# One left-over block product by seven products: a half-width node in the feed-forward stage of a recurrent block, with its sums on GpSimd

## The chip, the core and the metric

The kernel runs on one NeuronCore of a Trainium2 chip. The metric is the device time of one execution in microseconds (us); smaller is better. Beside the times of plain runs there is one profiled execution, whose trace names every instruction by the line of the kernel that issued it (L783 is line 783). The engines are TensorE (PE in the profile, its weight loads PEld), VectorE (DVE), ScalarE (ACT), GpSimd (POOL) and SyncE (SP, which issues most DMAs).

## The reference

Input x is 8 x 1024 x 512 in float32 (8 batches). All arithmetic is float32.

```python
xn = layernorm(x)
s  = attention(xn)            # recurrent, three decays, gated; times Wo and a scale
gate = xn @ lut[gate_idx].T   # 512 -> 1376
up   = xn @ lut[up_idx].T     # 512 -> 1376
h    = silu(gate) * up
g    = silu(h @ lut[down_idx].T)   # 1376 -> 512
out  = x + s * g
```

The change lies in the products `gate` and `up`. Their 1376 output columns are 11 tiles: ten of 128 (0 to 9) and one of 96 (10).

## The kernel before

Phase 1 normalizes x, runs the attention and writes to HBM, for each batch, x transposed and its block sums (`xs_d`); on the way it looks up the three weight matrices and writes their block sums to HBM as well. Phase 2 goes through the eight batches. For each one it computes gate and up (`quads`, and `single` for tile 10), then the down projection (`down`) and the output. In batch 0 `single` comes before `quads`; in batches 1 to 7 it comes after.

**Products of blocks.** Gate and up together are a 2 x 2 block product in the scheme of Strassen and Winograd: seven block products, numbered 1 to 7, in place of eight, with sums of the results. Each of the seven is itself done by seven products of smaller blocks. Such an inner scheme is a `Node`: it has four results in four PSUM banks (`t[0]` to `t[3]`, of the roles s11, s12, s21, sE) and adds its seven products into them. A quad is four output tiles. For the two quads (tiles 0 to 3 and 4 to 7) a node holds two weight tiles side by side, and goes through the block products 1, 6, 5, 7, 2, 3, 4 in seven nodes, `(1, 1)` to `(4, 4)`.

**The pair.** Tiles 8 and 9 are a pair. Here the two halves of a node are two different block products: `(1, 6)`, `(5, 7)` and `(2, 3)`, in that order. The seventh one left, block product 4, is no node. `Fourth` computes it without an inner scheme: two results of two matmuls of 512 columns each (L826), which DVE adds to the pair's `u3` (L835). It needs the x blocks of 4 as they were, which is why `restore` (L853) brings the second x block of product 4 back after the last node of the second quad.

**The order.** Every engine runs its instructions in the order in which they are traced (`keep_order`). The loop of `quads` interleaves each node with the first two steps of the one that follows, so that PE has the matmuls of the follower while ACT and DVE work on the results of the node:

```python
node.sixth()               # PE product 6; ACT copies t1 to t2 (L805); DVE t1 += e (L806)
node.product(0, 2); empty(node.t, 0)
if following: following.first()          # PE product 1; ACT copies t0 to t1 (L794)
node.seventh(); empty(node.t, 3)         # PE product 7, needs L805; DVE t3 = t2 + e (L810)
node.product(1, 3); empty(node.t, 1)     # PE product 3, needs L806
if following: following.fifth(); following.fifth_copy()   # PE product 5; ACT L801
if node.restores: restore(...)           # a DMA from ACT's queue
node.product(2, 4); empty(node.t, 2)     # PE product 4, needs L810
if after: after()                        # GpSimd
```

The matmuls of a node are L783: two matmuls of 256 columns a product, and each float32 matmul shows as two instructions of PE, so a product is four. `Fourth` stands in this loop as the follower of `(2, 3)`: its two results take the places of `first` and `fifth`; the first of its DVE adds (L835) stands ahead of L810, the second ahead of the adds for t2. After `(2, 3)` comes `single` (L721 to L758), or in batch 0 the first node of `down` (`DownNode`: L1037, L1059, L1066, L1070).

**What `empty` and `after` do for the pair.** Node (1, 6): ACT copies to p1 (L915), DVE adds to u2 (L916). Node (5, 7): ACT copies to e5 (L919), DVE adds to u3 (L920), GpSimd adds e5 to u2 (L921); after it GpSimd adds u3 to e5 (L931). Node (2, 3): DVE adds into p1 (L924) and into h (L926, needs L921), ACT applies Silu to both (L925, L927); after it GpSimd multiplies h by u3 and by e5 (L936).

**Weights.** A ring of three slots holds the weights of a node (L774 for the quads, L777 twice for a pair's node, 448 KB each; L819 twice for `Fourth`, 128 KB each; L721 for `single`; L1028 for `down`). The DMA of one starts when the one three places earlier has been read for the last time.

**Sums for the down projection.** `at_last` puts up to six DVE sums (L1005) into this loop in batch 0, two of them in node (5, 7) and three in (2, 3), one ahead of L810; in the other batches they lie in `single`.

Of the kernel before, what the change touches and what calls it, by code (L numbers as in the profile page):

```python
# [9 lines left out]
F32 = mybir.dt.float32  # L10
# [4 lines left out]
ALU = mybir.AluOpType  # L15
AX = mybir.AxisListType

P = 128
# [30 lines left out]
def recurrent_block(ctx: ExitStack, tc, x, wq, wk, wv, wo, wg, decay_logits, out_scale, lut, gidx, uidx, didx, out):  # L49
# [19 lines left out]
    nc = tc.nc  # L69
# [5 lines left out]
    U = 512  # L75
# [5 lines left out]
    NK = (NO - 1) // 2  # L81
    NQ = NO // 4
# [7 lines left out]
    wgu_d = [dram.tile([P, 14, m], F32, name=f"wgud{o}", tag=f"wgud{o}") for o, (_, m) in enumerate(OCH)]  # L90
# [42 lines left out]
    def defer(parts, issue):  # L133
        later.append([parts, issue])
# [111 lines left out]
    def ffn_weights(build, pool, pair_pool):  # L246
# [9 lines left out]
        def gate_up(o):  # L256
            s, m = OCH[o]
            n = 2 * NV * m
            idx = build.tile([P, NB], I32, name="idx", tag="idx", bufs=2)
            iv = idx[:, :n].rearrange("p (a b) -> p a b", b=m)  # L260
            gs, us = (src[:, s : s + m].rearrange("(c p) b -> p c b", p=P) for src in (gidx, uidx))
            nc.sync.dma_start(out=iv[:, 2:6, :], in_=gs)
            nc.sync.dma_start(out=iv[:, 0:2, :], in_=us[:, 0:2, :])
            nc.sync.dma_start(out=iv[:, 6:8, :], in_=us[:, 2:4, :])
            yield
            wf = pool.tile([P, 2 * NB], F32, name="wgu", tag="wgu", bufs=2)
            yield from look_up(build, wf[:, :n], idx[:, :n], P, n)
            w = wf[:, : 2 * n].rearrange("p (k two m) -> p k two m", two=2, m=m)
            a21, a11, a12, a22, s1, s2, s3, s4 = (w[:, k] for k in range(8))
            nc.gpsimd.tensor_tensor(s1, a21, a22, ALU.add)  # L270
            nc.gpsimd.tensor_tensor(s2, s1, a11, ALU.subtract)
            yield
            nc.gpsimd.tensor_tensor(s3, a11, a21, ALU.subtract)
            nc.gpsimd.tensor_tensor(s4, a12, s2, ALU.subtract)
            wide = wf[:, 2 * m : 2 * n].rearrange("p (a b) -> p a b", b=m)
            if o >= 4 * NQ:
                defer(3, lambda: nc.sync.dma_start(out=wgu_d[o], in_=wide))
            if o >= 2 * NK:
                return
            if o % 2 == 0:  # L280
                upper.append(w[:, 1:])
                return
            up, low = upper.pop(), w[:, 1:]
            to = quad_d[o // 4][:, :, o // 2 % 2, :].rearrange("p k (t m) -> p k t m", m=P)
            pair = pair_pool.tile([P, 7, 4, P], F32, name="pair", tag="pair")
            nc.sync.dma_start(out=to[:, :, 0:2, :], in_=up)
            defer(3, lambda: nc.sync.dma_start(out=to[:, :, 2, :], in_=low[:, :, 1, :]))
            b21, b22, b11, b12 = low[:, :, 0], low[:, :, 1], up[:, :, 0], up[:, :, 1]
            nc.gpsimd.tensor_tensor(pair[:, :, 0], b21, b22, ALU.add)
            yield  # L290
            nc.gpsimd.tensor_tensor(pair[:, :, 1], pair[:, :, 0], b11, ALU.subtract)
            yield
            nc.gpsimd.tensor_tensor(pair[:, :, 2], b11, b21, ALU.subtract)
            yield
            nc.gpsimd.tensor_tensor(pair[:, :, 3], b12, pair[:, :, 1], ALU.subtract)
            defer(4, lambda: nc.sync.dma_start(out=to[:, :, 3:7, :], in_=pair))
            for _ in range(3):
                yield
# [377 lines left out]
    W_OF = {1: 0, 2: 1, 4: 2, 5: 3, 6: 4, 7: 5, 3: 6}  # L676
    X_OF = {1: 0, 2: 1, 3: 2, 5: 3, 6: 4, 7: 5, 4: 6}
    D_OF = {1: 0, 7: 1, 2: 2, 3: 3, 5: 4, 6: 5, 4: 6}
    H = U // 2
    ORDER = (1, 6, 5, 7, 2, 3, 4)  # L680

    def phase_2():
        with (
# [12 lines left out]
            def bank(role, name):  # L696
                return psp.tile([P, U], F32, name=name, tag=role)
# [62 lines left out]
            class Node:  # L760
# [2 lines left out]

                def __init__(self, b, q, ks, xs):
                    self.ks, self.xs = ks, xs

                    self.restores = ks if q == NQ else (4,) if (q, ks) == (NQ - 1, (4, 4)) else ()
                    name = f"{b}_{q}_{ks[0]}"  # L770
                    self.w = ring.tile([P, 2, 7, P], F32, name=f"wq{name}", tag="wr")
                    w = self.w.rearrange("p a t m -> p a (t m)")
                    if q < NQ:
                        nc.sync.dma_start(out=w, in_=quad_d[q][:, W_OF[ks[0]], :, :])  # L774
                    else:
                        for a, k in enumerate(ks):
                            nc.sync.dma_start(out=w[:, a, :], in_=quad_d[q][:, W_OF[k], 0, :])  # L777
                    self.t = [bank(r, f"{r}{name}") for r in ("s11", "s12", "s21", "sE")]
                    self.name = f"e{name}"

                def product(self, n, i, start=False):
                    for a in range(2):
                        nc.tensor.matmul(  # L783
                            self.t[n][:, ts(a, H)],
                            lhsT=self.w[:, a, (0, 1, 6, 2, 3, 4, 5)[i - 1], :],
                            rhs=self.xs[:, X_OF[self.ks[a]], D_OF[i], :],
                            start=start and a == 0,
                            stop=False,
                            skip_group_check=True,
                        )  # L790

                def first(self):
                    self.product(0, 1, True)
                    nc.scalar.copy(self.t[1], self.t[0])  # L794

                def fifth(self):
                    self.product(3, 5, True)
                    self.e = tmp.tile([P, U], F32, name=self.name, tag="e")

                def fifth_copy(self):  # L800
                    nc.scalar.copy(self.e, self.t[3])  # L801
# [6 lines left out]
                def seventh(self):  # L808
                    self.product(2, 7)
                    nc.vector.tensor_tensor(self.t[3], self.t[2], self.e, ALU.add)  # L810

            class Fourth:


                def __init__(self, b, xs, u3):
                    self.b, self.xs, self.u3 = b, xs, u3
                    self.w = ring.tile([P, 14, P], F32, name=f"w4{b}", tag="wr")
                    for r in range(2):
                        nc.sync.dma_start(  # L819
                            out=self.w[:, ts(r, 2), :], in_=wgu_d[4 * NQ + r][:, ts(W_OF[4], 2), :]  # L820
                        )

                def product(self, r, role):
                    ps = bank(role, f"{role}{self.b}_4_{r}")
                    for n in range(2):
                        nc.tensor.matmul(  # L826
                            ps,
                            lhsT=self.w[:, 2 * r + n, :],
                            rhs=self.xs[:, X_OF[4], ts(n, 2), :],
                            start=n == 0,  # L830
                            stop=n == 1,
                            skip_group_check=True,
                        )
                    o = self.u3[:, ts(r, 2), :]
                    return lambda: nc.vector.tensor_tensor(o, ps.rearrange("p (a t) -> p a t", a=2), o, ALU.add)  # L835

                def first(self):
                    self.product(0, "s11")()

                def fifth(self):  # L840
                    self.add = self.product(1, "sE")

                def fifth_copy(self):
                    self.add()

            def quads(b, xs, h, sums, at_last):

# [53 lines left out]
                def pair_steps():  # L901
# [2 lines left out]
                        (t[:, :, :H], t[:, :, H:])  # L904
                        for t in (tmp.tile([P, 4, U], F32, name=f"{k}{b}_l", tag=k) for k in ("p1", "u2"))
                    )
                    room[0] = u3

                    def of_h(half, n):
                        r, c = divmod(n, 2)  # L910
                        t = half * U + c * H
                        return h[:, 4 * NQ + r, t : t + H]
# [20 lines left out]
                    def after_23():  # L933
                        for half, other in ((0, u3), (1, e5)):
                            for n in (0, 3, 1, 2):
                                nc.gpsimd.tensor_tensor(of_h(half, n), of_h(half, n), other[:, n], ALU.mult)  # L936

                    yield (1, 6), node_16, None
                    yield (5, 7), node_57, after_57
                    yield (2, 3), node_23, after_23  # L940

                room = [None]
                def every():
                    for q in range(NQ):
                        for ks, empty, after in steps(q):
                            yield Node(b, q, ks, xs), empty, after
                    for ks, empty, after in pair_steps():
                        yield Node(b, NQ, ks, xs), empty, after
                    yield Fourth(b, xs, room[0]), None, None
                    yield None, None, None  # L950

                todo = every()
# [288 lines left out]
            xs = room_for_x(0)  # L1241
# [92 lines left out]
```

## Time and profile before

| | |
|---|---|
| median of 3 runs | 2119.46 us (2119.22 to 2119.74) |
| the profiled execution | 2119.36 us, its span 2117.6 us |
| PE busy | 2109.2 us, 100% of the span |
| PEld busy | 1678.6 us, 79% |
| DVE, POOL, ACT busy | 1409.2, 1021.2, 929.4 us |
| HBM traffic | 282.87 MB read, 76.55 MB written |
| granted TensorE clock | 1.00 |

Busy is the time in which an engine has an instruction in work. The span runs from the first to the last instruction of the core; 1.76 us of the profiled execution's time lie outside it. A row of groups gives line, engine, operation, output<-inputs, shape and count, then busy us, mean ns of one, and the idle time of the engine ahead of them with what ended it.

### The profile page before, as it was taken

To read this page: it belongs to the slowest core of one execution; us is meant where nothing else is said; L and a number is where in the kernel's file an instruction comes from. 1 tells how busy PE (TensorE), PEld (TensorE's weight loads), DVE (VectorE), ACT (ScalarE), POOL (GpSimd) and SP (SyncE) were. 2 spreads that over 40 slices of the span, in tenths; PEclk is the share of its full clock that TensorE was granted. 3 is DMA by queue.
4 is the path that set the end of the run, shared out by engine and by line. 5 is a ranking of instruction groups with operands and counts; after the bars stand their busy time and mean duration, and the time that the engine had idled before them with its cause. 6 is when DMAs were issued, how large, how long until landed. Compare 5 with 4: busy or idle time off the path is not lost.

```text
span 2117.6 us, 31134 instructions
## 1 busy us (share of the span) xinstructions
PE 2109.2 (100%) x11306; PEld 1678.6 (79%) x11306; DVE 1409.2 (67%) x2150; ACT 929.4 (44%) x2083; POOL 1021.2 (48%) x1046
## 2 busy tenths in 40 slices
PE   9999999999999999999999999999999999999999
PEld 6666666666678888887879888887978888797877
DVE  6889888678545774576567556656755665675557
ACT  3666666666434414423441442344145324423531
POOL 2554565253354537416642752655275255527432
PEclk9999999999999999999999999999999999999999
DMA  7556557565464644464455446444544634464442
GB/s 195 158 176 160 190 174 169 181 129 177 110 252 153 240 168 153 156 236 140 146 195 185 151 148 245 139 147 172 208 151 154 246 123 155 165 218 148 152 154 109
DMA packets 164271, 361.45 MB, mean 171 GB/s; under 512 B 52083, under 2 KB 90230, under 8 KB 163094
## 3 DMA queue, kind: packets, MB, share of 16 engines
q1 hardware_dynamic: 149702, 336.12, 48.7%
q0 software_dynamic: 4480, 14.68, 1.7%
q10 hardware_dynamic: 9936, 8.66, 1.4%
q8 instruction: 90, 1.47, 0.3%
q14 instruction: 63, 0.52, 0.1%
HBM read 282.87 MB, written 76.55 MB: 170 GB/s over the span
## 4 chain that ended last, share of the span: by engine, by line
PE 98%; DVE 1%; DMA 1%; POOL 0%; issue 0%; ACTq 0%; ACT 0%; SPq 0%; POOLq 0%; DVEq 0%
PE s L783 33%; PE pq L455 10%; PE pv L418 8%; PE sE L783 6%; PE s12d L1037 5%; PE s21d L1037 5%; PE s11d L1037 5%; PE po L583 4%; PE fs L731 3%; PE pd L1145 3%; PE ps L1152 3%; PE sEd L1037 2%; PE psc L561 2%; PE pu L569 2%; PE pt L411 1%; PE fsE L731 1%
## 5 line engine op out<-in xcount | busy, mean ns | idle before, releaser
L783 PE MATMUL s<-xs,wq 128*128 128x256 f32 x3264 | 731.2, 379 | 0.0
L783 PEld LDWEIGHTS s<-xs,wq 128*128 128x128 f32 x3264 | 619.6, 190 | 95.8 <-issue 8.1
L806 DVE TENSOR_TENSOR s<-s,e 128x512 f32<-128x512 f32 x136 | 95.1, 699 | 204.1 <-ACT s L805 204.0
L455 PE MATMUL pq<-xnT,wqk_sb 128*128 128x512 f32 x512 | 230.3, 592 | 0.0
L1116 POOL TENSOR_TENSOR cu<-cu 128x256 f32<-128x256 f32 x32 | 34.8, 1088 | 306.7 <-DVE cl L1115 306.7
L418 PE MATMUL pv<-wvg_sb,xnT 128*128 128x387 f32 x512 | 177.6, 489 | 0.3 <-DMA wvg_sb<-in_wv 0.3
L714 POOL TENSOR_TENSOR xs<-xs 128x256 f32<-128x256 f32 x224 | 170.8, 789 | 4.5
L455 PEld LDWEIGHTS pq<-xnT,wqk_sb 128*128 128x128 f32 x512 | 92.4, 190 | 92.1 <-issue 91.8
L810 DVE TENSOR_TENSOR sE<-s,e 128x512 f32<-128x512 f32 x136 | 95.0, 699 | 104.9 <-PE s L783 104.9
L874 POOL TENSOR_TENSOR u<-u,e 128x512 f32<-128x512 f32 x64 | 79.9, 1270 | 148.7 <-DVE u L870 130.2
L801 ACT COPY e<-sE 128x512 f32<-128x512 f32 x136 | 79.6, 585 | 138.8 <-PE sE L783 138.5
L783 PE MATMUL sE<-xs,wq 128*128 128x256 f32 x544 | 139.6, 379 | 0.0
L397 POOL TENSOR_SCALAR rstd<-rstd 128x1 f32<-128x1 f32 x56 | 27.8, 497 | 229.6 <-ACT junk L396 229.0
L418 PEld LDWEIGHTS pv<-wvg_sb,xnT 128*128 128x128 f32 x512 | 92.7, 190 | 54.8 <-issue 2.4
L878 POOL TENSOR_TENSOR h<-h,u 128x512 f32<-128x512 f32 x64 | 80.1, 1272 | 113.1 <-DVE u L885 103.5
L794 ACT COPY s<-s 128x512 f32<-128x512 f32 x136 | 77.5, 570 | 109.2 <-PE s L783 105.1
L805 ACT COPY s<-s 128x512 f32<-128x512 f32 x136 | 77.5, 570 | 97.6 <-PE s L783 97.6
L1037 PE MATMUL s12d<-wdd,z 128*128 128x128 f32 x896 | 118.5, 275 | 0.6 <-ACT s12d L1059 0.6
L783 PEld LDWEIGHTS sE<-xs,wq 128*128 128x128 f32 x544 | 103.4, 190 | 14.0
L1037 PEld LDWEIGHTS s12d<-wdd,z 128*128 128x128 f32 x896 | 109.1, 192 | 0.8 <-ACT s12d L1059 0.8
L224 DVE TENSOR_SCALAR leaf<-idx,lut_x,lut_sb 128x1024 int32<-128x1024 int32 (+2 forms) x119 | 101.3, 876 | 0.0
L563 DVE TENSOR_TENSOR pr<-psc,w_tab 128x384 f32<-128x384 f32 x64 | 35.5, 555 | 92.0 <-PE psc L561 91.8
(236 smaller groups left out, 4254.3 us busy)
## 6 DMA issues: line engine op xcount, KB each, us to landing
wq<-quadd SPq DMA_DIRECT2D x112, 896.0 KB, 4.5
wdd<-wdd SPq DMA_DIRECT2D x56, 896.0 KB, 4.8
xs<-xsd SPq DMA_DIRECT2D x56, 512.0 KB, 6.6
wq<-quadd SPq DMA_DIRECT2D x48, 448.0 KB, 4.1
x<-in_x SPq DMA_DIRECT2D x64, 256.0 KB, 5.9
xsd<-ts SPq DMA_DIRECT2D x8, 2048.0 KB, 7.5
gx<-in_x SPq DMA_DIRECT2D x64, 256.0 KB, 5.4
out<-gx POOLq DMA_DIRECT2D x56, 256.0 KB, 2.3
```

The lines of the kernel that those rows point to most:

```text
L224: nc.vector.tensor_scalar(o.bitcast(I32), iv, lut_x[:rows, k, :], lut_i[:rows, k, 0:1], ALU.bitwise_and, ALU.bitwise_xor,)
L418: nc.tensor.matmul(pv, lhsT=xnT[:, v, ts(c, P)], rhs=wvg_sb[:, v, :], start=(v == 0), stop=(v == NV - 1))
L455: nc.tensor.matmul(pq, lhsT=wqk_sb[:, v, ts(j, D)], rhs=xnT[:, v, ts(hf, U)], start=(v == 0), stop=(v == NV - 1))
L583: nc.tensor.matmul(po, lhsT=lh, rhs=rh, start=(n == 0), stop=(n == len(prods) - 1))
L714: nc.gpsimd.tensor_tensor(o, x1, x2, ALU.subtract)
L731: nc.tensor.matmul(ps, lhsT=w[:, 2 * W_OF[k] + n, :m], rhs=xs[:, X_OF[k], 2 * n : 2 * n + 2, :], start=start and n == 0, stop=stop and n == 1,
L783: nc.tensor.matmul(self.t[n][:, ts(a, H)], lhsT=self.w[:, a, (0, 1, 6, 2, 3, 4, 5)[i - 1], :], rhs=self.xs[:, X_OF[self.ks[a]], D_OF[i], : ...
L806: nc.vector.tensor_tensor(self.t[1], self.t[1], self.e, ALU.add)
L810: nc.vector.tensor_tensor(self.t[3], self.t[2], self.e, ALU.add)
L874: nc.gpsimd.tensor_tensor(o[:, n], o[:, n], other[:, n], ALU.add)
L878: nc.gpsimd.tensor_tensor(of_h(half, n), of_h(half, n), two(other[:, n]), ALU.mult)
L1037: nc.tensor.matmul(self.t[n][:, ts(a, P)], lhsT=self.lhs[i][:, e, ts(a, P)], rhs=self.w[:, e, D_OF[i], :], start=start and a == 0 and e == ...
```

## The change

Block product 4 of the pair becomes a `Node` of its own, `(4,)`, half as wide as the others: seven products of one matmul of 256 columns. It stands between `(5, 7)` and `(2, 3)`. ACT copies its four results to a new tile `m4`, and GpSimd adds them to u3. `Fourth` goes away, and `(2, 3)` has no follower in the loop any more. The restore of x's block for product 4 moves from the second quad's last node to the new node; its weights are one DMA of 448 KB from `quad_d`, and phase 1 no longer writes tiles 8 and 9 to `wgu_d` (`OCH` tiles at or above `2 * NK` = 10 remain).

```diff
-            if o >= 4 * NQ:
+            if o >= 2 * NK:
                 defer(3, lambda: nc.sync.dma_start(out=wgu_d[o], in_=wide))
...
-                    self.restores = ks if q == NQ else (4,) if (q, ks) == (NQ - 1, (4, 4)) else ()
+                    self.restores = ks if q == NQ else ()
...
-                    self.t = [bank(r, f"{r}{name}") for r in ("s11", "s12", "s21", "sE")]
+                    self.n = len(ks) * H
+                    self.t = [bank(r, f"{r}{name}")[:, : self.n] for r in ("s11", "s12", "s21", "sE")]
...
-                    for a in range(2):
+                    for a in range(len(self.ks)):
...
-                    self.e = tmp.tile([P, U], F32, name=self.name, tag="e")
+                    self.e = tmp.tile([P, U], F32, name=self.name, tag="e")[:, : self.n]
...
-            class Fourth:
...
-                    room[0] = u3
+                    m4 = tmp.tile([P, 4, H], F32, name=f"m4{b}", tag="m4")
...
+                    def node_4l(t, n):
+                        nc.scalar.copy(m4[:, n], t[n])
+
+                    def after_4l():
+                        for n in (0, 3, 1, 2):
+                            nc.gpsimd.tensor_tensor(u3[:, n], u3[:, n], m4[:, n], ALU.add)
+
                     yield (1, 6), node_16, None
                     yield (5, 7), node_57, after_57
+                    yield (4,), node_4l, after_4l
                     yield (2, 3), node_23, after_23
...
-                    yield Fourth(b, xs, room[0]), None, None
                     yield None, None, None
```

More of the change, by code (lines that the diff above doesn't have):

```diff
@@ L810, in seventh @@
                     nc.vector.tensor_tensor(self.t[3], self.t[2], self.e, ALU.add)
-            class Fourth:
[L815 to L844, printed above, removed]
             def quads(b, xs, h, sums, at_last):
@@ L936, in after_23 @@
                                 nc.gpsimd.tensor_tensor(of_h(half, n), of_h(half, n), other[:, n], ALU.mult)
+                    def node_4l(t, n):
[3 more added lines that the diff above has]
+                            nc.gpsimd.tensor_tensor(u3[:, n], u3[:, n], m4[:, n], ALU.add)
                     yield (1, 6), node_16, None
                     yield (5, 7), node_57, after_57
+                    yield (4,), node_4l, after_4l
                     yield (2, 3), node_23, after_23
-                room = [None]
                 def every():
```

## The prediction

> **What bounds the kernel now.** I read the page first, then PE's waits, then the timeline of one pair (batch 1) and of batch 0's, then the groups by shape. The page, and PE's waits (who waited <- for whom: us in total, times, longest):
>
> ```profile
> PE 2109.2 (100%) x11306; PEld 1678.6 (79%) x11306; DVE 1409.2 (67%) x2150; ACT 929.4 (44%) x2083; POOL 1021.2 (48%) x1046
> ...
> PE 98%; DVE 1%; DMA 1%; POOL 0%; issue 0%; ACTq 0%; ACT 0%; SPq 0%; POOLq 0%; DVEq 0%
> ```
>
> ```profile
> PE s12d L1037 <- ACT s12d L1059: 0.6, 1, 0.6
> PE s11d L1048 <- DVE sx L1005: 0.4, 1, 0.4
> ```
>
> PE is never without work for long: 98% of the chain is PE, and the waits it has in the feed-forward stage are two, both in batch 0's down projection. So a matmul that goes shortens the time by its full length, if nothing new makes PE wait. The rows of batch 1's pair (start, length, instruction, idle before it and its releaser):
>
> ```profile
> 893.92 0.57 ACT L805 COPY s<-s 128x512 f32<-128x512 f32 x1 [0.55 <-PE s L783]
> ...
> 894.52 0.70 DVE L806 TENSOR_TENSOR s<-s,e 128x512 f32<-128x512 f32 x1 [0.69 <-ACT s L805]
> 894.53 1.88 PE L826 MATMUL s<-xs,w 128*128 128x512 f32 x4
> ...
> 895.13 0.41 DVE L924 TENSOR_TENSOR p_l<-s,p_l 128x256 f32<-128x256 f32 x1
> ...
> 895.46 0.41 DVE L926 TENSOR_TENSOR h<-s,p_l 128x256 f32<-128x256 f32 x1
> ...
> 896.25 1.89 PE L783 MATMUL s<-xs,wq 128*128 128x256 f32 x8
> ...
> 897.33 0.69 DVE L810 TENSOR_TENSOR sE<-s,e 128x512 f32<-128x512 f32 x1
> ...
> 897.97 1.88 PE L826 MATMUL sE<-xs,w 128*128 128x512 f32 x4
> ...
> 899.69 1.03 PE L783 MATMUL s<-xs,wq 128*128 128x256 f32 x4
> ```
>
> `Fourth` is seen to do two things. It computes, and it lies between product 2 and product 7 of (2, 3), and between products 3 and 4, where L805 and L810 must end first.
>
> **What goes from PE.** From the start of L826 to that of the next product is 896.25 - 894.53 = 1.72 us, and again 899.69 - 897.97 = 1.72: 3.43 us a batch with the third digit (429 ns an instruction). The node that comes has 7 products of 2 instructions. Batch 1's (2, 3) begins at 892.80 and L826 follows 8 instructions on, at 894.53, so one takes 216 ns, and 14 take 3.02 us. The gain is 0.41 us a batch, 3.3 us in eight.
>
> **What covered (2, 3) and is gone.** Let (2, 3) begin at 0 (892.80 before). Product 6 is issued until 0.86, product 2 until 1.73. L805 starts at 1.12 and ends at 1.69. Where PE does wait in this trace, its weight load starts 0.05 us behind the releaser's end and the next matmul is 0.10 us late on top (batch 0: ACT ends at 725.25, the load is at 725.30, the following matmuls are 0.21 apart once, then 0.11). Hence product 7 can run from 1.69 + 0.15 = 1.84 in place of 1.73: a stall of 0.12 us. Without `Fourth`, product 7's results come at 1.84 + 1.03 = 2.87, but DVE is busy: L806 from 1.72, L924 and L926 until 895.88 - 892.80 = 3.07 (successive DVE rows overlap by 0.08). L810 runs from 2.99 to 3.68, and product 4, which needs it, from 3.68 + 0.15 = 3.83. Products 7 and 3 end at 1.84 + 1.73 = 3.57: a stall of 0.26 us. Product 3 needs L806 (2.42) and gets it in time. So (2, 3) loses 0.38 us of the 0.41 us; a batch from 1 to 7 gains 0.03 us, and seven of them 0.2 us.
>
> **The new node's own waits.** Nodes (5, 7) and (4,) overlap their followers as before, with less to lie under: between products 2 and 7 of (5, 7) PE has 0.43 us where it had 0.86. L805 of (5, 7) ends at 888.45, and product 7 would start at 888.92 with its load at 888.70; L810 then ends at 890.68 and product 4's load is at 890.86. Both just hold, by 0.2 and 0.1 us. In (4,) the copy and the two adds are of 256 columns; the rows nearest are those of `down`, of that shape:
>
> ```profile
> L1071 DVE TENSOR_TENSOR s12d<-s12d,ed 128x256 f32<-128x256 f32 x56 | 23.9, 428 | 54.7 <-ACT s21d L1070 53.9
> ...
> L931 POOL TENSOR_TENSOR u_l<-u_l 128x256 f32<-128x256 f32 x32 | 22.2, 725 | 0.0
> ...
> L1070 ACT COPY s21d<-s12d 128x256 f32<-128x256 f32 x56 | 20.0, 357 | 88.7 <-PE s12d L1037 88.7
> ```
>
> Product 6 of (4,) ends 0.6 us after its start; the copy ends at 1.05 and product 7 is due at 1.73, behind (2, 3)'s first product. It holds with 0.5 us. DVE does two adds of 0.43 us, where L835 took two of 0.69: 0.5 us less. ACT gets three copies more of 0.36 and four of 0.37 to m4, 2.6 us in a stretch of 3.9 us in which it otherwise has two copies of 0.57 and 0.59; the last of them ends 0.4 us before L805 of (2, 3) starts. The moved restore sits in ACT's queue ahead of the m4 copy of t2 (issue 0.37 us, beside ACT's work). What it waits for is the new node's product 7 and DMAs landed long before, and nobody reads its block until `single`'s last product, 14 us on. So zero; if the restore held ACT up by 0.5 us, L805 of (2, 3) and then PE would be 0.2 us late.
>
> **GpSimd.** Four adds of 0.73 us come in front of L936. m4 is complete at 0.75 us into (2, 3), and GpSimd has the adds done at about 3.3, as the first Silu of (2, 3) is (3.2). The multiplies then follow the Silus, as now, and end near where they ended (906.1), 7 us ahead of the down projection. The Trainium skill's page GPSIMD Engine Reference (section 4.1, Engine selection) speaks against such a placing: elementwise work belongs on VectorE, GpSimd being about twice as slow for two inputs. The rows agree on the ratio (725 against 415 to 428 ns); still no term of the sum changes, since on DVE the four adds would take 1.7 us in (4,), where it is idle for over 2 us. The same page (section 8, Key points) has the two engines contend when DVE reads two inputs from SBUF; batch 0 shows it: an L1005 sum takes 1.10 us beside GpSimd's adds and 0.68 alone.
>
> **Batch 0.** It has L1005 sums in the loop, and `down` directly behind.
>
> ```profile
> 715.94 0.71 DVE L1005 TENSOR_TENSOR z<-z,h 128x512 f32<-128x512 f32 x1
> ...
> 719.93 0.68 DVE L1005 TENSOR_TENSOR z<-h 128x512 f32<-128x512 f32 x1
> ...
> 725.30 0.94 PE L1037 MATMUL s12d<-wdd,z 128*128 128x128 f32 x6 [0.61 <-ACT s12d L1059]
> ```
>
> The second sum now falls ahead of L806 of (4,), whose product 3 is thereby 0.35 us late; the third lies between L926 and L810 of (2, 3), and product 4 loses 0.75 us, by the order above with the sum's 0.6 us added. Then DVE's adds for t2 end at 725.34 (724.53 before), two Silus and L1059 follow, and product 6 of `down` starts 0.8 us later than it did. There the wait swallows the gain. I take +0.8 us (bounds +0.2, if the sums find gaps, and +1.6, if both are slowed to 1.1).
>
> **DMAs.** The weights of (2, 3) start when (1, 6) ends (886.95) and are wanted at 892.6; before, it was 880.91 and 887.4. They landed 4.7 us after the first issue, at most 5.7; the restore of (1, 6) beside it is 128 KB larger than the one that was there. It holds with 0.5 us or more, so zero. Phase 1 writes two times 896 KB less and waits for none of it: zero, or up to 0.5 us of gain.
>
> **Sum.** 2119.36 - 0.2 + 0.8 = 2120.0 us, 0.5 us above the median of the runs.
>
> **Rivals.**
> - *The cover is not missed.* If DVE gets L810 in ahead (or the pipeline forgives it), all 3.3 us stay and batch 0 loses nothing: 2116.1; with batch 0's two present waits (0.6 and 0.4 us) gone too, 2115.1. For it: the stalls computed are a quarter of a us each, made of rows' differences. Against it: L806, L924 and L926 are queued ahead of L810 by order. Chance 0.10.
> - *(2, 3) waits for its weights*, the case on the slow side. The lead falls to 5.65 us because only a half node's matmuls lie in between. It decides once the landing takes longer than that. L721's weights land in 5.0 to 6.3 us after issue; at 6.3 the price is 0.65 us x 8 = 5.2 and the time 2125.2. Against it: these are the 4.7 us rows. Chance 0.13.
> - *The last node is uncovered by a whole DVE operation more*: if L810 or an m4 copy falls one place later in its queue than I have it, (2, 3) loses 0.7 us more in each batch: 2120 + 5.6 = 2125.6. Chance 0.13.
> - That the node is not run as said is excluded: the order of PE's instructions has 14 in the place named.
>
> **Numbers.** A measurement of this kernel can tell about 0.2% (4.2 us) from no change: 2115.2 to 2123.7. The forecast (0.64) has 2118 to 2122.5, by restart costs between 0.05 and 0.25 us a stall and batch 0's bounds. The first rival mostly stays within 4.2 us. Faster 0.06, same 0.70, slower 0.24. The range 2116.2 to 2125.2 takes in both ends but the tails.
>
> **What would show it.** In the profile after, L826 and L835 are gone; PE has 14 instructions more a pair of about 216 ns; two waits of PE stand in (2, 3), on L805's and L810's successors, of about 0.1 and 0.3 us; a larger one in batch 0's L1037 product. The forecast is wrong if the weights' DMA is named as a releaser of PE, if (4,) itself makes PE wait in batches 1 to 7, or if no wait stands in (2, 3).

## The result, and the profile after

The changed kernel takes 2124.91 us (median of 8 runs, 2123.38 to 2127.96), the kernel before 2119.34 beside it (8 runs, 2119.15 to 2119.74). The ratio is 1.0027, with a 95% interval of 1.0016 to 1.0038: 5.6 us slower. That is inside the range given, but outside the forecast's own 2118 to 2122.5; the likeliest side, "within 0.2%", was not the one, though the interval still touches 0.2%. The profiled execution took 2123.75 us with a span of 2122.0, 4.39 us more than the one before, so what the trace accounts for below is about 1 us less than what the median shows.

The page's busy line and its chain of waits, of the changed kernel:

```profile
PE 2110.3 (99%) x11354; PEld 1685.4 (79%) x11354; DVE 1405.1 (66%) x2150; ACT 948.6 (45%) x2139; POOL 1044.5 (49%) x1078
...
PE 94%; DMA 3%; DVE 2%; ACT 1%; POOL 0%; issue 0%; SPq 0%; ACTq 0%; POOLq 0%; DVEq 0%
```

Before, PE had 98% of the chain and DMA 1%. DMA now has 3%: in places the chain runs through a transfer where it ran along PE. PE's waits say which transfer:

```profile
PE fs L731 <- DMA xs<-xsd: 2.0, 7, 0.4
...
PE s L785 <- DVE sE L812: 1.0, 1, 1.0
PE s12d L1010 <- ACT s12d L1032: 0.8, 1, 0.8
PE s L785 <- DMA wq<-quadd: 0.5, 1, 0.5
```

Seven times `single` (L731) waits for a transfer of x blocks: once in batch 0, as before (0.2), and once in each of the batches 2 to 7. Batch 1 has the same wait, too short for this view, which counts only time in which PE is wholly idle. In the text below a stall is taken from the starts of the matmuls, against the same pair of instructions elsewhere, and is larger. The other three rows are all batch 0's; the last is the weights of `(2, 3)`. Lines have shifted: L785, L796, L807, L808, L812 are the old L783, L794, L805, L806, L810; `restore` is L821, the DVE adds L891 and L893, the sums for `down` L978, its weights L1001, its matmuls and first copy L1010 and L1032.

The timeline of batch 1, from the middle of `(2, 3)` to tile 10's product 2 (start, length, instruction, idle before it and its releaser):

```profile
896.87 5.02 SPq L1001 DMA_DIRECT2D wdd<-wdd  x2
...
897.32 2.79 POOL L910 TENSOR_TENSOR u_l<-u_l,m 128x256 f32<-128x256 f32 x4
897.79 0.57 ACT L807 COPY s<-s 128x512 f32<-128x512 f32 x1 [0.44 <-PE s L785]
898.40 0.70 DVE L808 TENSOR_TENSOR s<-s,e 128x512 f32<-128x512 f32 x1 [2.81 <-ACT s L807]
898.41 1.59 PEld L785 LDWEIGHTS s<-xs,wq 128*128 128x128 f32 x8 [0.25 <-ACT s L807]
899.00 0.41 DVE L891 TENSOR_TENSOR p_l<-s,p_l 128x256 f32<-128x256 f32 x1
899.33 0.41 DVE L893 TENSOR_TENSOR h<-s,p_l 128x256 f32<-128x256 f32 x1
...
899.67 0.69 DVE L812 TENSOR_TENSOR sE<-s,e 128x512 f32<-128x512 f32 x1
...
900.05 0.74 POOL L903 TENSOR_TENSOR h<-h,u_l 128x256 f32<-128x256 f32 x1
...
900.41 0.73 PEld L785 LDWEIGHTS s<-xs,wq 128*128 128x128 f32 x4 [0.40 <-DVE sE L812]
...
901.84 0.42 ACT L894 ACTIVATE h<-h 128x256 f32<-128x256 f32 x1
901.90 0.37 ACTq L821 DMA_DIRECT2D xs<-xsd  x1
...
906.81 0.24 PEld L731 LDWEIGHTS fs<-xs,wr 128*96 128x96 f32 x2 [0.97 <-ACT fs L745]
906.84 1.50 PE L731 MATMUL fs<-xs,wr 128*96 128x512 f32 x3
```

Three things are to be seen. The two weight loads of L785 that wait, at 898.41 and 900.41, are the two predicted stalls of `(2, 3)`; each comes 0.05 us behind its releaser's end. GpSimd's four adds (L910) end at 900.11, and its first multiply (L903) follows at once. And the restore of `(2, 3)`'s x blocks, which tile 10's product 2 reads as they were, is issued at 901.90; product 2 was due at 906.5 and starts at 906.84. The releaser that PEld's row names, L745, had ended at 906.38; PE's row above names the right one. The same stretch before:

```profile
899.51 0.42 ACT L927 ACTIVATE h<-h 128x256 f32<-128x256 f32 x1
899.57 0.37 ACTq L853 DMA_DIRECT2D xs<-xsd  x1
...
899.88 1.18 SPq L1028 DMA_DIRECT2D wdd<-wdd  x2
...
905.70 1.88 PE L731 MATMUL fs<-xs,wr 128*96 128x512 f32 x4
```

The DMA issues of the same stretch (KB, median us from issue to landing), before and then after:

```profile
wdd<-wdd SPq DMA_DIRECT2D x2, 896.0 KB, 5.7
xs<-xsd ACTq DMA_DIRECT2D x1, 256.0 KB, 2.8
```

```profile
wdd<-wdd SPq DMA_DIRECT2D x2, 896.0 KB, 5.5
...
xs<-xsd ACTq DMA_DIRECT2D x1, 256.0 KB, 4.8
```

The restore took 2.8 us and now takes 4.8, so it lands at 906.70. Before, it was issued at 899.57 for a product 2 at 905.70: a lead of 6.1 us for 2.8. After, the lead is 4.6 us for 4.8.

The lead is shorter because of what stands ahead of the restore in ACT's queue. In both traces it goes out 0.06 us behind the start of the last Silu of `t[1]` (L927 before, L894 after), and the Silus wait for DVE's adds. Before, `Fourth`'s second result kept PE at work between products 3 and 4 while they ran, and the restore went out 0.12 us ahead of product 4's start (899.69). After, product 4 starts at 900.41 and the restore follows 1.49 us later.

The landing is longer because the restore now goes out behind a load of `down`'s weights (L1001, 896 KB each). The two loads are issued at 896.87 and 901.57; before, at 899.88 and 900.75, both behind the restore. The first moved because it waits for the last matmul of `(4,)` where it waited for that of `Fourth`. The second follows the start of the last matmul of `(2, 3)` by 0.41 us in both traces, and it is the second that holds the restore. From 902 to 905 us the trace has 121 packets of SP's queue starting (0.85 MB) and none of ACT's; the restore's first packet starts 3.2 us after its issue, where it was 1.0 us before. It is 3.1 to 3.4 us in all seven batches, and 1.0 in all seven before.

The Trainium skill's page DMA: Bandwidth & Descriptors (section Queues, rings and completion order) has each DMA engine take turns between the queues that have work for it, and change only when it has drained a whole packet of some 9 to 17 descriptors. In the trace, ACT's queue got its turn when the load issued 0.33 us ahead was nearly through. The two fit if a DMA engine's share of that load (128 rows of 7 KB over 16 engines, so 8 rows, as an estimate) is one such packet, which no run here shows.

In batch 0, the rows of the stalls, same view:

```profile
715.68 1.56 PE L785 MATMUL s<-xs,wq 128*128 128x256 f32 x6 [0.48 <-DMA wq<-quadd]
...
721.37 1.07 DVE L978 TENSOR_TENSOR z<-h 128x512 f32<-128x512 f32 x1
...
722.36 0.68 DVE L812 TENSOR_TENSOR sE<-s,e 128x512 f32<-128x512 f32 x1
...
723.10 1.13 PE L785 MATMUL s<-xs,wq 128*128 128x256 f32 x4 [0.99 <-DVE sE L812]
...
726.81 1.16 PE L1010 MATMUL s12d<-wdd,z 128*128 128x128 f32 x8 [0.80 <-ACT s12d L1032]
```

The second half of the weights of `(2, 3)` lands 6.5 us after its issue at 709.13, while three loads for the down projection go out beside it from 709.62 on. The sum L978 takes 1.07 us ahead of L812.

**Where the 4.39 us are**, by the starts of matmuls in the two traces: phase 1 -0.40; batch 0 +1.23; batches 1 to 7 without the restore -0.2 (the stalls in `(2, 3)` are 0.385 us a batch, PE's gain 0.41); the restore +3.36 (seven waits of 0.31 to 0.61, 3.02 together, with 0.05 of restart each); behind the last matmul +0.37. Together +4.4.

### The profile page after: what moved, and what is told of

Read it like the earlier page. It is cut to its first block, busy times and chain, and to the rows that moved or that the text cites. A ratio compares the mean times of both kernels' runs of the same rounds, so it can differ in the third digit from the quotient of the medians.

```text
span 2122.0 us, 31352 instructions
## 1 busy us (share of the span) xinstructions
PE 2110.3 (99%) x11354; PEld 1685.4 (79%) x11354; DVE 1405.1 (66%) x2150; ACT 948.6 (45%) x2139; POOL 1044.5 (49%) x1078
## 4 chain that ended last, share of the span: by engine, by line
PE 94%; DMA 3%; DVE 2%; ACT 1%; POOL 0%; issue 0%; SPq 0%; ACTq 0%; POOLq 0%; DVEq 0%
PE s L785 33%; PE pq L455 10%; PE pv L418 8%; PE sE L785 6%; PE s12d L1010 5%; PE s21d L1010 5%; PE s11d L1010 5%; PE po L583 4%; PE pd L1118 3%; PE ps L1125 3%; PE sEd L1010 2%; PE fs L731 2%; PE psc L561 2%; DMA xs<-xsd 2%; PE pu L569 2%; PE pt L411 1%
## 5 line engine op out<-in xcount | busy, mean ns | idle before, releaser
L785 PE MATMUL s<-xs,wq 128*128 128x256 f32 x3360 | 754.0, 380 | 1.5 <-DVE sE L812 1.0
L785 PEld LDWEIGHTS s<-xs,wq 128*128 128x128 f32 x3360 | 636.3, 190 | 97.8 <-DVE sE L812 4.2
L808 DVE TENSOR_TENSOR s<-s,e 128x512 f32<-128x512 f32 x144 | 98.6, 685 | 221.0 <-ACT s L807 221.0
L812 DVE TENSOR_TENSOR sE<-s,e 128x512 f32<-128x512 f32 x144 | 98.5, 684 | 108.7 <-PE s L785 108.7
L785 PE MATMUL sE<-xs,wq 128*128 128x256 f32 x560 | 144.4, 379 | 0.0
L796 ACT COPY s<-s 128x512 f32<-128x512 f32 x144 | 80.4, 558 | 110.7 <-PE s L785 107.6
L807 ACT COPY s<-s 128x512 f32<-128x512 f32 x144 | 80.4, 558 | 96.5 <-PE s L785 95.8
L1010 PE MATMUL s12d<-wdd,z 128*128 128x128 f32 x896 | 118.4, 275 | 0.8 <-ACT s12d L1032 0.8
L785 PEld LDWEIGHTS sE<-xs,wq 128*128 128x128 f32 x560 | 106.4, 190 | 14.5
L1010 PEld LDWEIGHTS s12d<-wdd,z 128*128 128x128 f32 x896 | 109.0, 192 | 1.0 <-ACT s12d L1032 1.0
```

Of the source, the lines that this page charges most:

```text
L785: nc.tensor.matmul(self.t[n][:, ts(a, H)], lhsT=self.w[:, a, (0, 1, 6, 2, 3, 4, 5)[i - 1], :], rhs=self.xs[:, X_OF[self.ks[a]], D_OF[i], : ...
L807: nc.scalar.copy(self.t[2], self.t[1])
L808: nc.vector.tensor_tensor(self.t[1], self.t[1], self.e, ALU.add)
L1010: nc.tensor.matmul(self.t[n][:, ts(a, P)], lhsT=self.lhs[i][:, e, ts(a, P)], rhs=self.w[:, e, D_OF[i], :], start=start and a == 0 and e == ...
```

## The experiments

Each kernel is the changed one with the edit shown, unless said otherwise; times are medians of 11 runs, ratios are to the kernel before on the same chip.

**1 and 2. The restore, issued earlier, or left out.** The theory: the loss is the restore of `(2, 3)` that `single` waits for. The rivals: GpSimd's adds, or batch 0 alone.

```diff
                     node.seventh()
+                    if node.ks == (2, 3):
+                        restore(2, 3)
                     empty(node.t, 3)
...
-                    if node.restores:
+                    if node.restores and node.ks != (2, 3):
                         restore(*node.restores)
```

The second kernel has only the lower half of this edit, so the blocks stay as `(2, 3)` left them.

> The changed kernel, with the restore of blocks 2 and 3 issued right behind product 7 of node (2, 3), ahead of the Silus in ACT's queue. Theory A (the restore comes late for tile 10's product 2, behind the down projection's weights; node (2, 3) is uncovered; batch 0 loses apart): the seven waits of L731 on the restore go, 3.0 us in the profile and more in the median, so 2120.5 to 2122 us with a narrower spread; the waits in (2, 3) stay at 0.37 us a batch. Theory B (GpSimd's adds and the longer queue of GpSimd are what costs): unchanged, 2124 to 2126 us.

> The changed kernel without the restore of blocks 2 and 3 (left out; tile 10's products 2 and 3 then use altered blocks in batches 1 to 7). Theory A: within 0.5 us of the kernel with the early restore, 2120.3 to 2121.8 us, as nothing is left to wait for. If that kernel is slower than this one by more, an early restore still collides with the weights. Theory B: 2124 to 2126 us.

Issued earlier: 2119.85 us, ratio 1.0002 (0.9993 to 1.0011). Left out: 2120.17, ratio 1.0002 (0.9993 to 1.0011). PE's wait, and the transfer in batch 1's stretch, of the kernel with the early issue:

```profile
PE fs L731 <- DMA xs<-xsd: 0.2, 1, 0.2
```

```profile
xs<-xsd ACTq DMA_DIRECT2D x1, 256.0 KB, 4.2
```

The seven waits are gone in both (what is left is one in batch 0's loads, which the kernel before has too), while the two stalls in `(2, 3)` stay as they were. The transfer still takes 4.2 us, but with a lead of 6.7 it is in time. The early issue, ahead of the Silus in ACT's queue, is at 899.17, 1.7 us ahead of the second load of `down`, while the first still goes out as early as in the changed kernel (896.17). So the restore makes the whole difference between the changed kernel and the one before, and the rest of the change is worth nothing that these runs can tell. Both came out below the time expected: batch 0's wait on weights was smaller too, 0.15 and 0.30 us in place of 0.64, though no edit touches those loads.

**3. The sums of the new node on DVE.** DVE adds from PSUM into `u3`; no `m4`, no copies to it, no GpSimd adds.

```diff
                     def node_4l(t, n):
-                        nc.scalar.copy(m4[:, n], t[n])
-
-                    def after_4l():
-                        for n in (0, 3, 1, 2):
-                            nc.gpsimd.tensor_tensor(u3[:, n], u3[:, n], m4[:, n], ALU.add)
+                        nc.vector.tensor_tensor(u3[:, n], t[n], u3[:, n], ALU.add)
...
-                    yield (4,), node_4l, after_4l
+                    yield (4,), node_4l, None
```

> The changed kernel with the four adds of node (4,) done by DVE straight from PSUM: no m4, no ACT copies to it, no adds on GpSimd. Theory A: GpSimd's adds are covered and cost nothing, so 2124 to 2126 us as the changed kernel; DVE may wait for GpSimd's sums of u3 into e5, which would add up to 0.5 us a batch. Theory B: 2 to 4 us come back, 2121 to 2123 us.

2125.16 us, ratio 1.0030 (1.0021 to 1.0039), like the changed kernel's 1.0027, and the same wait:

```profile
PE fs L731 <- DMA xs<-xsd: 2.1, 8, 0.3
```

GpSimd's sums cost nothing, and neither do ACT's copies for them: that rival falls.

**4. The kernel before, with its cover taken away.** `Fourth` stays as it was, but runs behind `(2, 3)` and no longer inside it.

```diff
+                    if node.ks == (2, 3):
+                        fourth = Fourth(b, xs, room[0])
+                        fourth.first()
+                        fourth.fifth()
+                        fourth.fifth_copy()
                     if after:
                         after()
...
-                    yield Fourth(b, xs, room[0]), None, None
```

> The kernel before, with the two results of block product 4 computed behind node (2, 3) instead of inside it; same matmuls. Theory A (the cover is worth 0.37 us a batch): the waits on L805 and L810 appear in (2, 3), 7 x 0.37 = 2.6 us plus 0.3 to 1 us in batch 0: 2122.2 to 2123 us. Without a cover's worth: 2119.3 us. The restore is not late here, as 3.4 us of matmuls still lie ahead of tile 10.

2122.67 us, ratio 1.0017 (1.0008 to 1.0025). PEld's waits, and the restore in batch 1's stretch:

```profile
PEld s L783 <- DVE sE L810: 4.3, 8, 1.5
...
PEld s L783 <- ACT s L805: 2.0, 8, 0.3
```

```profile
xs<-xsd ACTq DMA_DIRECT2D x1, 256.0 KB, 7.4
```

Both waits stand in `(2, 3)`, and by the matmuls' starts they cost the same 0.385 us a batch in batches 1 to 7 as in the changed kernel. This is the price of the cover by itself: 2.95 us by the medians, where eight times 0.385 is 3.1. Here the weights of `down` are issued 0.4 us ahead of the restore, and it takes 7.4 us; nobody waits, since `Fourth` and `single` leave it a lead of 8.0. So a late landing alone does no harm. It needs the short lead as well.

**5. A longer lead, by tile 10's own order.** The restore is as late as in the changed kernel, but `single` does product 7 before product 2.

```diff
-                product(pa, 2, False, True)
-                nc.scalar.activation(sg, pa, AF.Silu)
                 product(pc, 7, False, False)
                 nc.vector.tensor_tensor(u3, pc, e, ALU.add)
+                product(pa, 2, False, True)
+                nc.scalar.activation(sg, pa, AF.Silu)
                 at_last(1)
```

> The changed kernel with its late restore, but tile 10's products in the order 1, 6, 5, 7, 2, 3, 4 (7 ahead of 2): product 2 is due 1.72 us later, 6.3 us behind the restore's issue, and the restore lands 4.8 to 5.1 us behind it. Theory A: the waits on the restore go with nothing done to the restore itself, 2119.9 to 2120.8 us (up to 0.1 us a batch may come back as product 7 waiting for ACT's copy). If the restore costs by its DMA's collision with other traffic rather than by product 2's wait for it: 2124 to 2126 us.

2122.76 us, ratio 1.0018 (1.0010 to 1.0027): 2 us under the changed kernel, but not the time expected. In six of the seven batches the wait is gone, and the pitch from batch to batch is 188.27 us (188.29 before), so the lead is what decides. In batch 4 a wait of 0.73 is left. There the restore and the second load of `down` took 7.0 us each. The rest of the miss is the edit's own: batch 0 runs the same `single`, and there x's blocks arrive in the old order.

```profile
PE fs L731 <- DMA xs<-xsd: 3.4, 2, 2.8
```

The 2.8 of this row is that wait, up to 611.5 us. It cost more than its length: behind it the granted TensorE clock reads 0.50 from 612.6 to 616.0 us, and matmuls of 512 columns start up to 0.85 us apart where it was 0.43, which is 1.7 us more.

**6 to 9. The cover given back.** With the restore early, the pair's last node gets a follower again: in batches 1 to 7 tile 10's products 1 and 6 stand where `Fourth`'s two results stood, and its products 5, 7, 2, 3, 4 follow (`Single`). The second kernel also lets the first node of `down` follow in batch 0. The third has no follower, but batch 0's loads of `down`'s small weights go out a quad earlier. The fourth has all three.

```diff
-                    yield None, None, None
+                    yield last(), None, None
...
+                def last():
+                    if b:
+                        return Single(b, NO - 1, xs, h_tail, at_last)
+                    return DownNode(b, 1, blocks(h)[0], got[0])   # None in the first kernel
...
+                            if (b, q, ks) == (0, 1, (1, 1)):       # third and fourth
+                                hold(out=wd_left, in_=wdl_d.rearrange("p (k o) -> p k o", o=H))
+                                hold(out=wd_tail[: OCH[-1][1], :], in_=wdt_d)
```

> The changed kernel with the early restore, and in batches 1 to 7 tile 10's products 1 and 6 as the follower of node (2, 3), its other products in the order 5, 7, 2, 3, 4. Theory A: the waits of 0.37 us a batch in (2, 3) go, 7 x 0.37 = 2.6 us below the kernel with the early restore alone (2119.85): 2117.2 us, faster than the kernel before by 2.4 us. If the stalls in (2, 3) are only moved into tile 10: 2119.5 to 2120 us.

> As the run with tile 10 as follower, and in batch 0 the first node of the down projection as the follower of (2, 3). Theory A: batch 0's waits on L812 (0.8 us) and on the down projection's first copy (1.0 us) shrink, 0.8 to 1.6 us less: 2115.6 to 2116.4 us. If batch 0 is held by DVE's sums as a whole, the wait only moves behind: 2117.2 us.

> The changed kernel with the early restore, and batch 0's loads of the down projection's small weights (1.1 MB) moved from behind the pair's weights to the start of the second quad. Theory A: the wait of (2, 3) for its weights in batch 0 (0.25 to 0.75 us with its restart) goes: 2119.2 to 2119.7 us. If that wait is not from these loads: 2119.85 us.

> Everything together: early restore, followers in all batches, early loads. Theory A: 0.3 us below the run with both followers, 2115.3 to 2116.2 us, the 3.3 us of matmuls saved nearly whole.

| | median | ratio |
|---|---|---|
| follower in batches 1 to 7 | 2118.27 | 0.9994 (0.9985 to 1.0003) |
| follower in all | 2118.38 | 0.9994 (0.9985 to 1.0003) |
| loads earlier | 2121.03 | 1.0006 (0.9997 to 1.0015) |
| all three | 2118.70 | 0.9994 (0.9985 to 1.0002) |

All four lie above what theory A gave, and none is told from the kernel before; the runs of that kernel themselves went from 2118.77 to 2123.81 here. The traces say more. With the follower no wait is left in `(2, 3)`, but tile 10's weights are wanted a node sooner, and a new wait shows (first kernel):

```profile
PE fs L776 <- DMA wr<-wgud: 0.8, 1, 0.8
```

With the follower in batch 0 too, the waits on L812's successor and on `down`'s first copy go, and one of 1.4 us on the sum `sx` appears in the down projection; batch 0 takes 178.16 us in this trace, against 178.42 with the early restore alone, and the medians show no gain. The earlier loads did not take batch 0's wait on weights away: 0.18 us of it stands in the third kernel's trace, as 0.15 with the early restore alone, and batch 0 takes 178.42 us in both. So the runs don't show that those two loads held the weights. The third kernel's profiled run lost 2.3 us in phase 1, which the edit does not touch.

**10 and 11. Tile 10's weights in four DMAs**, the blocks of products 1 and 6 first: once with all three edits, once with the follower in batches 1 to 7 alone.

```diff
-                    nc.sync.dma_start(out=self.w[:, :, :m], in_=wgu_d[o])
+                    for k, n in ((0, 2), (8, 10), (2, 8), (10, 14)):
+                        nc.sync.dma_start(out=self.w[:, k:n, :m], in_=wgu_d[o][:, k:n])
```

> Early restore, followers in all batches, early loads of batch 0, and tile 10's weights loaded by four DMAs, those of products 1 and 6 first. Theory A: the scattered waits for tile 10's weights (0.1 to 1.1 us in a profile) go, and the waits in (2, 3) stay away: 2116 to 2117.5 us, 0.5 to 1.5 us below the run with one DMA, faster than the kernel before by 2 to 3 us. If the single-DMA waits were not the cause of its scatter: 2118.5 us.

> Early restore, tile 10 as the follower in batches 1 to 7 with its weights in four DMAs; batch 0 as in the changed kernel. Theory A: 0.37 x 7 = 2.6 us below the kernel with the early restore alone, and free of waits for weights: 2117 to 2117.8 us.

All: 2116.68 us (2116.62 to 2117.24), ratio 0.9989 (0.9980 to 0.9998). The second: 2117.11 us, ratio 0.9991 (0.9982 to 1.0000). The first is the version to keep, 2.5 us under the kernel before and some 8 under the changed one. What the four DMAs add by themselves is not shown, as the interval overlaps that of the same kernel with one DMA (0.9985 to 1.0002). Its batch 1, timeline:

```profile
897.44 1.88 PE L777 MATMUL fs<-xs,wr 128*96 128x512 f32 x4
...
899.16 1.89 PE L839 MATMUL s<-xs,wq 128*128 128x256 f32 x8
...
900.22 0.37 ACTq L875 DMA_DIRECT2D xs<-xsd  x1
...
900.88 1.88 PE L777 MATMUL fs<-xs,wr 128*96 128x512 f32 x4
...
902.60 1.03 PE L839 MATMUL s<-xs,wq 128*128 128x256 f32 x4
903.46 1.88 PE L777 MATMUL fsE<-xs,wr 128*96 128x512 f32 x4
905.18 3.17 PE L777 MATMUL fs<-xs,wr 128*96 128x512 f32 x7
```

Tile 10's matmuls (L777) lie between the products of `(2, 3)` (L839) as `Fourth`'s did, and the starts are 1.72 us apart, which is four instructions of 429 ns or eight of 216 (0.86 for the four at 902.60): nothing is lost. The restore is issued 6.7 us ahead of its reader (product 2 follows product 7, which starts at 905.18) and landed in 2.5 us, with the first load of `down` all but through and the second not yet issued. PE's waits in the feed-forward stage are down to two of batch 0, besides two of 0.4 and 0.2 us in `single` at the start of phase 2:

```profile
PE s11d L1081 <- DVE sx L1038: 1.2, 1, 1.2
...
PE s L839 <- DVE s L862: 0.2, 1, 0.2
```

## Why the prediction was right and wrong

**The gain and the loss of cover: right.** The new node runs in 216 ns an instruction and makes no wait in batches 1 to 7. Product 7 of `(2, 3)` is 0.12 us late and product 4 0.27, as worked out from L805's, L806's and L810's rows (0.12 and 0.26); DVE's order L808, L891, L893, L812 is the one assumed. Batches 1 to 7 would gain 0.025 us each, and with the restore early they do (188.27 us from batch to batch, 188.29 before). The fourth experiment shows the loss alone, the tenth and eleventh what the matmuls give when it is avoided: 2.5 and 2.0 of the 3.3 us.

**"DMAs" priced at zero: wrong, and the main miss.** That step went through the weights of `(2, 3)` and the restores of `(1, 6)` and of the new node. It left out the restore of `(2, 3)`, which the diff does not touch and which the change moves twice: nearer to its reader, since the Silus ahead of it in ACT's queue lost `Fourth`'s cover as well, and behind the second load of `down`'s weights, 0.33 us after it where it was 1.18 us ahead. Before, its slack was 3.3 us in batch 1 (a lead of 6.1 against 2.8); the lead lost 1.5 and the landing gained 2.0. The missing term measured 3.36 us in the profiled execution, and about 5 in the medians (1.0027 against 1.0002). Without it the kernel takes 2119.85 us, beside a sum of 2120.0. That 2124.91 still lies in the range given is luck: its upper end was set by a transfer that was not the one.

**Batch 0: mis-sized.** +0.8 was forecast, +1.23 measured, within its bounds of +0.2 to +1.6. Product 4's part was 1.26 in place of 0.75, with the sum at 1.07 us. Product 3 of `(4,)` did not wait by itself, since `(2, 3)` was late anyway for its weights. And `down`'s product 6 waited 1.06 us where it had waited 0.88, while a wait of 0.66 on a later sum (`sx`) is gone.

**The rivals.** "`(2, 3)` waits for its weights" happened, in batch 0 only, for 0.64 us; at 2125.2 its time is near the one measured, but by another transfer in another place. With it came one of the signs given for a wrong forecast: the weights' DMA is named as a releaser of PE. "The cover is not missed" fell, in this kernel. So did "a whole DVE operation more": no add or copy came later in its queue than it was put. GpSimd was right at zero, to the tenth of a us at which its adds end beside the first Silu.

**Phase 1** was 0.40 us shorter, but not by the writes it lost: a wait at about 9 us, at its very start, is 0.56 us in the trace of before and 0.13 after. The traces of experiments 2 and 11, which lose the same writes, begin the quads of batch 0 at 616.45 and 616.43 us, as the one before does (616.45).

**What stays open.** The plain runs of the changed kernel lie 4.6 us apart, those of the one before 0.6. The third experiment, with the same late restore, scatters by 5.9, the fourth, whose restore lands 0.6 us ahead of its reader, by 5.4, the first and second by 1.5 and 2.3. That fits a transfer that lands at the edge of its lead, but the plain runs have no trace, and the kernel before scattered by 5.0 us too beside experiments 6 to 9. Nor do the runs say why the DMA engines nearly finish a load of 896 KB before they turn to ACT's queue, or what held the weights of `(2, 3)` in batch 0.

## What to carry to other kernels

When an edit shortens the work between two points, list every transfer that is issued ahead of that stretch and read behind it, those that the diff doesn't mention included, and compare lead and landing for each. The lead starts where the transfer is issued, so look at what stands ahead of it in its engine's queue, and at which loads it will now go out behind. Work that computes little may still be cover: price what each instruction hides before it is taken out, and look for other work (here the next tile's first products) that can be put in its place. A new follower brings its own operands forward, and these may have to be loaded in the order in which they are now read.

## What the runs showed of the hardware

A 256 KB transfer on ACT's queue landed, in batches 1 to 7, in 2.6 to 3.0 us (once 5.1) when issued ahead of two loads of 896 KB on SP's (the kernel before); in 2.5 to 3.2 with the first all but through and the second not yet issued (experiment 10); in 4.8 to 5.0 when issued 0.33 to 0.61 us behind the second (the changed kernel); in 2.9 to 4.3 with the first under way and the second issued 1.7 us behind it (experiment 1); and in 5.2 to 7.4 when issued 0.4 us behind the first (experiment 4). Its first packet started 1.0 us after the issue in the first two cases and 3.1 to 3.4 us after it in the third.

Behind a wait of PE of 2.8 us (experiment 5) the granted clock reads 0.50 for 3.4 us; in the other traces, where PE waits for at most 1.6 us at a time behind the first 8 us, it stays at 1.00 until the matmuls end.

In `(2, 3)` a stalled product's weight load started 0.05 us behind the end of what released it, and the matmul after the first was 0.10 us late on top; in tile 10's product 2, of 512 columns, that was 0.05. From the last matmul to the end of the span it is 5.08 us in the two traces with `Fourth`, and 5.42 to 5.53 in the eleven with the new node, although nothing there was changed; the cause stays open.
